# A cross-attention block on one core: a ring for the softmax weights, values copied by ScalarE, one DMA queue

## The chip, the core and the metric

The kernel runs on one core of a Trainium2 chip. TensorE (PE in the profile) multiplies matrices, VectorE (DVE) and GpSimd (POOL) work on elements, reductions and small transposes, ScalarE (ACT) does activations and copies, and DMA transfers are issued by SyncE (SP) or by ScalarE. Each engine runs its own instructions in the order in which they were written and waits for the others at semaphores. The metric is device time in microseconds (us) for one execution; lower is better.

## The reference

The input is x and a context c, each 128 sequences of 128 tokens with 256 features, in fp32. For each sequence the reference computes one cross-attention block with 16 heads of 16 features and a feed-forward layer of 1024:

```python
q = x @ Wq + bq;  k = c @ Wk + bk;  v = c @ Wv + bv        # 16 heads of 16
scores = q @ k.T / sqrt(16)
scores = where(j < i, scores, -1e30)                       # strictly below the diagonal
attn = softmax(scores);  attn[..., 0, :] = 0
x1 = layer_norm(x + (attn @ v) @ Wo + bo, ln1_g, ln1_b)
out = layer_norm(x1 + relu(x1 @ W1 + b1) @ W2 + b2, ln2_g, ln2_b)
```

## The kernel before

Two sequences make a pair, so there are 64 pairs. Several pairs are in flight at once: the main loop's `step(p)` (lines 988 to 1042, p from 5 to 63) computes the scores and the softmax of pair p, weighs the values of pair p-2 and takes them through the output projection and the first norm, runs the feed-forward layer of pair p-3, starts the second norm of pair p-4 and finishes and stores pair p-5. Nothing reorders the work: the order of calls in `step` is the order on each engine. Pairs 0 to 4 go through written-out openings (the last of them are `third`, `fourth` and `fifth`), and the last pairs through a written-out tail from line 1050 on.

On PE a step is: `weigh(p-2)` (lines 464 and 474), `scores_both(p)` (line 357), `queries(p+1)` and `keys(p+1)` (line 257), with `attention_out(p-2)` (line 493) between them, `values(p)` (line 289), `hidden(p-3)` (line 680) and `second(p-3)` (line 698). All eight PSUM banks are assigned by hand. Two assignments matter here. `second` leaves its result in bank 6, and the last part of the next step's `scores_both` writes to bank 6 too, so it cannot start before VectorE has read the result in `second_sum` (line 708). And `hidden` uses banks 2, 3, 4 and 0, which the next `scores_both` needs as well, so ScalarE must have run its Relu on them (line 686).

The scores are cut by query rows into a low half (rows 0 to 63 of each sequence, which see 64 keys) and a high half (rows 64 to 127, which see 128 keys). For each half VectorE adds the mask (`mask`, line 371) and takes the negated maximum (line 382), GpSimd adds it (line 383), ScalarE takes the exponential (line 390), VectorE sums and inverts (`sums`, lines 402 and 403) and GpSimd multiplies (line 404). The high half goes in two parts of eight heads, called ONE and TWO, the low half as a whole.

To weigh values, PE needs the weights turned, with keys on the partitions. VectorE transposes 32x32 blocks into a tile `tb` (`turn`, line 417, three instructions a pair), and sixteen DMA transfers then exchange the blocks between partition groups, from `tb` into `pT` (`bring`, line 432). The first-norm output takes a like road: a block transpose into `tbx` (`turn_x1`, line 644), four transfers to DRAM (line 235) and one back (line 238), for `hidden`.

The buffers: the scores have two tiles each for the low and high halves, `tb` one and `pT` one. So `turn(p)` must wait until `bring(p-1)` has read `tb`, and `bring(p-1)`, issued at the start of step p, may write `pT` only after `weigh(p-2)` has read it. `values_out` (lines 294 to 307) puts the values into zero-padded tiles: `vz` for the high rows and `vd` for the low ones, where the second head of a pair of heads lies on partitions 64 to 127. ScalarE copies the first half of `vd` from PSUM, and a DMA from `vz`, issued by ScalarE (line 303), fills the second half. `store` (line 587) is issued by ScalarE too. All other transfers of the loop are issued by SyncE.

The first norm's statistics are four VectorE instructions (`stats`, lines 506 and 507), a variance step on GpSimd (`deviation`, `shift`, lines 513, 514 and 558) and two ScalarE activations (`norm1`, line 535), which stand between the Relus of `hidden`. At two pairs `second` also issues idle PE instructions; that stays as it is.

Of the kernel before, what the change touches and what calls it, by code (L numbers as in the profile page):

```python
# [8 lines left out]
F32 = mybir.dt.float32  # L9
# [4 lines left out]
P = 128  # L14
# [5 lines left out]
def tile_cross_attention_block(  # L20
# [273 lines left out]
    def values_out(p):  # L294
        st = states[p]
        pv = st.pop("pv")
        st["vz"], st["vd"] = vzs[p % 2], vds[p % 2]
        for s in range(2):
            nc.scalar.copy(
                st["vz"][:, s, :, 0:4:3, :],  # L300
                pv[:, s * D : (s + 1) * D].rearrange("p (r e d) -> p r e d", e=2, d=DK),
            )
        nc.scalar.dma_start(st["vd"][HP:], st["vz"][:HP, :, :, 2:4, :])
        nc.scalar.copy(
            st["vd"][:HP, :, :, 0, :].rearrange("p s r d -> p (s r) d"),
            pv[:HP].rearrange("p (u e d) -> p u e d", e=2, d=DK)[:, :, 0, :],
        )

    def scores(p, hi):

        st = states[p]
        n = P if hi else HP
        sps = [at_bank(r, f"pss{hi}_{p}_{r}") for r in range(NS)]
        for m in range(KC):
            for s in range(2):
                first = s * P  # L320
                for r in range(NS):
                    strip = slice(32 * r, 32 * r + 32)
                    nc.tensor.matmul(
                        sps[r][
                            s * HP : (s + 1) * HP, m * 2 * n : (m + 1) * 2 * n
                        ].rearrange("p (e j) -> p e j", e=2),
                        st["qT"][strip, m, first + hi * HP : first + hi * HP + HP],
                        st["kT"][strip, m, :, first : first + n],
                        start=True, stop=True,
                    )  # L330
        st["sps", hi] = sps
        st["sm", hi] = soft.tile(
            [P, H, n], F32, tag=f"sm{hi}", name=f"sm{hi}_{p}", bufs=2
        )
        st["nmx", hi] = small.tile([P, H], F32, tag=f"nmx{hi}", name=f"nmx{hi}_{p}")

    def scores_both(p):

        st = states[p]
        for hi in range(2):  # L340
            st["sps", hi] = [
                at_bank(r if hi else (6, 7, 4, 5)[r], f"pss{hi}_{p}_{r}") for r in range(NS)
            ]
            st["sm", hi] = soft.tile(
                [P, H, P if hi else HP], F32, tag=f"sm{hi}", name=f"sm{hi}_{p}", bufs=2
            )
            st["nmx", hi] = small.tile([P, H], F32, tag=f"nmx{hi}", name=f"nmx{hi}_{p}")
        one, two = (0, 1), (2, 3)
        for strips, hi, m in (
            (two, 0, 0), (one, 1, 0), (two, 0, 1), (one, 1, 1),  # L350
            (two, 1, 0), (two, 1, 1), (one, 0, 0), (one, 0, 1),
        ):
            n = P if hi else HP
            for s in range(2):
                for r in strips:
                    strip, first = slice(32 * r, 32 * r + 32), s * P
                    nc.tensor.matmul(  # L357
                        st["sps", hi][r][
                            s * HP : (s + 1) * HP, m * 2 * n : (m + 1) * 2 * n
                        ].rearrange("p (e j) -> p e j", e=2),  # L360
                        st["qT"][strip, m, first + hi * HP : first + hi * HP + HP],
                        st["kT"][strip, m, :, first : first + n],
                        start=True, stop=True,
                    )
# [46 lines left out]
    def turn(p, hi, t):  # L411

        st = states[p]
        if "tb" not in st:
            st["tb"] = soft.tile([P, NS, (H + HH) * 32], F32, tag="tb", name=f"tb_{p}")
        at = (t if hi else 2) * 256
        nc.vector.transpose(  # L417
            st["tb"][:, :, at : at + 256].rearrange("p j (n a) -> p n j a", a=32),
            st["sm", hi].rearrange("p h j -> p (h j)")[:, t * 1024 : (t + 1) * 1024].rearrange(
                "p (n j a) -> p n j a", j=NS, a=32  # L420
            ),
        )

    def bring(p, queue, which):

        st = states[p]
        if "pT" not in st:
            pT = st["pT whole"] = soft.tile([P, NS, (H + HH) * 32], F32, tag="pT", name=f"pT_{p}")
            st["pT"] = pT.rearrange("p i (n a) -> p i n a", a=32)
        for u in which:  # L430
            i, j = u // NS, u % NS
            queue.dma_start(  # L432
                st["pT whole"][32 * j : 32 * j + 32, i, :], st["tb"][32 * i : 32 * i + 32, j, :]
            )

    def turn_on_pe(p, hi, ts):

        st = states[p]
        sm = st["sm", hi].rearrange("p h j -> p (h j)")
        if "pT" not in st:  # L440
            pT = soft.tile([P, NS, (H + HH) * 32], F32, tag="pT", name=f"pT_{p}")
            st["pT"] = pT.rearrange("p i (n a) -> p i n a", a=32)
        for t in ts:
            pt = bank(f"ptp{hi}_{p}_{t}")
            for i in range(4):
                at = (4 * t + i) * P
                nc.tensor.transpose(pt[:, i * P : (i + 1) * P], sm[:, at : at + P], ident)
            n = 4 * t if hi else H + 4 * t
            nc.scalar.copy(
                st["pT"][:, :, n : n + 4, :].rearrange("p i n a -> p n i a"),  # L450
                pt.rearrange("p (n i a) -> p n i a", i=NS, a=32),
            )
# [70 lines left out]
    def attention_stats(p):  # L523
        stats(p, states[p]["t1"], 1)
        deviation(p, 1)
# [58 lines left out]
        nc.vector.scalar_tensor_tensor(t2, t2, sd, be2_r, ALU.mult, ALU.add)  # L584

    def store(p):
        nc.scalar.dma_start(
            out[2 * p : 2 * p + 2].rearrange("b p d -> p b d"), states.pop(p)["t2"]
        )

# [323 lines left out]
    def fourth():  # L914
# [26 lines left out]
        turn(p, 1, 1)  # L941
        attention_out(p - 1)
        attention_sum(p - 1)
        sums(p, 0, ALL)
        attention_stats(p - 1)
        shift(p - 1, 1)
        tokens(p + 2, "x")
        keys(p + 1)
        turn(p, 0, 0)
        bring(p, nc.sync, LATE_FIRST)  # L950
        stats(0, states[0]["t2"], 2)
        scale_and_shift(0)
        norm1(p - 1)
        turn_x1(p - 1)
        hidden(1, range(FC))
        norm2(0)

    def fifth():
        p = 4
        load_ahead(p)  # L960
        scores_both(p)
        mask(p, 0, B)
        mask(p, 1, A)
        maximum(p, 1, ONE)
        queries(p + 1)
        mask(p, 1, B)
        maximum(p, 1, TWO)
        exponential(p, 1, ONE)
        mask(p, 0, A)
        maximum(p, 0, ALL)  # L970
        keys(p + 1)
        exponential(p, 1, TWO)
        values(p)
        values_out(p)
        sums(p, 1, ONE)
        exponential(p, 0, ALL)
        sums(p, 1, TWO)
        sums(p, 0, ALL)
        tokens(p + 2, "x")
        tokens(p + 2, "c")  # L980
        second(1, 0)
        second(1, 1)
        turn(p, 1, 0)
        turn(p, 1, 1)
        turn(p, 0, 0)
        hidden(2, range(FC // 2))

    def step(p):
# [1 line left out]
        weigh(p - 2)  # L990
        context(p - 2)
        scores_both(p)
        bring(p - 1, nc.sync, LATE_FIRST)
        load_ahead(p)
        second_sum(p - 4)
        residual1(p - 3)
        finish(p - 5)
        add_bo(p - 1)
        mask(p, 0, B)
        mask(p, 1, A)  # L1000
        maximum(p, 1, ONE)
        if not last:
            queries(p + 1)
        store(p - 5)
        attention_out(p - 2)
        mask(p, 1, B)
        maximum(p, 1, TWO)
        exponential(p, 1, ONE)
        mask(p, 0, A)
        maximum(p, 0, ALL)  # L1010
        if not last:
            keys(p + 1)
        exponential(p, 1, TWO)
        attention_sum(p - 2)
        values(p)
        stats(p - 4, states[p - 4]["t2"], 2)
        stats(p - 2, states[p - 2]["t1"], 1)
        scale_and_shift(p - 4)
        deviation(p - 2, 1)
        shift(p - 2, 1)  # L1020
        values_out(p)
        sums(p, 1, ONE)
        exponential(p, 0, ALL)
        sums(p, 1, TWO)

        def between(f):
            if f == 4:
                norm1(p - 2)

        hidden(p - 3, range(FC // 2 if p == 5 else 0, FC), between)  # L1030
        norm2(p - 4)
        sums(p, 0, ALL)
        if p + 2 < NP:
            tokens(p + 2, "x")
            tokens(p + 2, "c")
        turn(p, 1, 0)
        turn_x1(p - 2)
        turn(p, 1, 1)
        turn(p, 0, 0)
        pad = 7 if p in (28, 51) else 0  # L1040
        second(p - 3, 0, pad=pad)
        second(p - 3, 1, pad=pad)
# [7 lines left out]
    p = NP - 1  # L1050
    weigh(p - 1)
    context(p - 1)
    bring(p, nc.sync, LATE_FIRST)
    second_sum(p - 3)
    residual1(p - 2)
    finish(p - 4)
# [7 lines left out]
    scale_and_shift(p - 3)  # L1064
    store(p - 4)
    hidden(p - 2, range(2, FC), lambda f: norm1(p - 1) if f == 4 else None)
    turn_x1(p - 1, nc.scalar)
    norm2(p - 3)
    second(p - 2, 0)
    second(p - 2, 1)  # L1070
# [85 lines left out]
```

## Time and profile before

Three runs gave 1625.21, 1629.5 and 1635.55 us; the median is 1629.5 us.

| | |
|---|---|
| the profiled execution's own time | 1624.7 us |
| its span | 1623.0 us |
| PE busy, PE weight loads busy | 1588.8 us (98%), 1359.0 us (84%) |
| VectorE, GpSimd, ScalarE busy | 1266.6 us (78%), 1304.0 us (80%), 787.8 us (49%) |
| mean granted PE clock | 0.994 |
| DMA queue of SyncE, of ScalarE | 183.08 MB in 394912 packets, 26.50 MB in 86704 packets |
| VectorE idle before the turns (line 417) | 258.9 us |

The span is the time between the first and the last instruction in the trace. A matmul's end is modelled in the trace, and successive matmuls overlap, so PE's 98% is not a measure of how much work there was; the distance between the starts of the same instruction in two steps is the surer measure. In a list of waits, a line names the waiting engine and line, then what released it, then the total in us, the count and the longest. `PEld` is PE loading weights, and `SPq` is the queue of instructions by which SyncE issues transfers.

### The profile page before, as it was taken

The page shows a single profiled execution, that of the slowest core. Times are in us where ns is not written, and L with a number is a line of the kernel's source. Part 1 is how long each engine was busy: PE and PEld are TensorE (multiplying, and loading weights), DVE is VectorE, ACT ScalarE, POOL GpSimd, SP SyncE. Part 2 cuts the span into 40 slices and gives each one's busy share as a digit, 9 for nine tenths or more (in the row PEclk, how much of TensorE's full clock was granted, in tenths as well). Part 3 has the DMA queues.
Part 4 walks back from the last instruction along what each step waited for, and adds up shares of the span by engine and source line. Part 5 has one row for each costly group of instructions (what it writes and reads, how often), then busy time and mean ns, then how long its engine had stood idle before and what let it go on. Part 6 is the DMA issues. An engine that isn't in the chain of part 4 may idle for free.

```text
span 1623.0 us, 41609 instructions
## 1 busy us (share of the span) xinstructions
PE 1588.8 (98%) x16486; PEld 1359.0 (84%) x16486; DVE 1266.6 (78%) x2125; ACT 787.8 (49%) x1616; POOL 1304.0 (80%) x1229
## 2 busy tenths in 40 slices
PE   8989999999999999999999999999999999999998
PEld 7768888888888888888888888888888888888877
DVE  6967877878878778778778788787787787787852
ACT  5545445445445355354454454453554554544532
POOL 6859788788888787787887888887878878878873
PEclk9989999999999999999999999999999999999999
DMA  9435555565665665656655656656556656565541
GB/s 196 99 79 132 136 130 127 137 138 136 141 131 125 138 143 131 140 121 137 134 140 138 133 124 138 139 133 141 126 131 141 138 132 133 129 138 119 137 120 48
DMA packets 481809, 212.23 MB, mean 131 GB/s; under 512 B 349008, under 2 KB 449616, under 8 KB 481616
## 3 DMA queue, kind: packets, MB, share of 16 engines
q1 hardware_dynamic: 394912, 183.08, 50.3%
q10 hardware_dynamic: 86704, 26.50, 6.6%
q8 instruction: 131, 2.15, 0.6%
q14 instruction: 62, 0.51, 0.1%
HBM read 70.26 MB, written 33.29 MB: 64 GB/s over the span
## 4 chain that ended last, share of the span: by engine, by line
DVE 31%; DMA 16%; SPq 14%; PE 13%; ACT 13%; POOL 9%; issue 4%; DVEq 0%; ACTq 0%; POOLq 0%
SPq L432 14%; DVE tb L417 12%; DMA vd<-vz 9%; DVE sm L371 7%; DMA pT<-tb 6%; ACT sm L390 6%; POOL sm L383 6%; DVE nmx L382 5%; ACT kT L279 4%; PE ph L680 4%; PE py L698 3%; POOL sm L404 2%; DVE tbx L644 2%; DVE t L708 2%; DVE su L402 2%
## 5 line engine op out<-in xcount | busy, mean ns | idle before, releaser
L383 POOL TENSOR_TENSOR sm<-sm,nmx 128x1024 f32<-128x1024 f32 x192 | 364.3, 1898 | 234.2 <-DVE nmx L382 231.6
L680 PE MATMUL ph<-x1T,w 128*128 128x256 f32 x2048 | 455.8, 380 | 5.6 <-DMA x1T<-x1t 5.4
L698 PE MATMUL py<-w,hT 128*128 128x256 f32 x2016 | 446.1, 379 | 0.8 <-ACT hT L686 0.8
L680 PEld LDWEIGHTS ph<-x1T,w 128*128 128x128 f32 x2048 | 389.5, 191 | 60.8 <-issue 3.3
L698 PEld LDWEIGHTS py<-w,hT 128*128 128x128 f32 x2016 | 382.7, 190 | 54.3 <-ACT hT L686 2.4
L417 DVE STREAM_TRANSPOSE tb<-sm 128x1024 f32<-128x1024 f32 x186 | 221.9, 1217 | 258.9 <-DMA pT<-tb 142.6
L404 POOL TENSOR_TENSOR sm<-sm,rs 128x1024 f32<-128x1024 f32 x192 | 359.3, 1898 | 5.6 <-DVE rs L403 5.4
L371 DVE TENSOR_TENSOR sm<-pss,neg 128x512 f32<-128x512 f32 (+1 forms) x512 | 253.4, 545 | 17.6 <-PE pss L357 13.6
L390 ACT ACTIVATE sm<-sm 128x1024 f32<-128x1024 f32 x192 | 203.3, 1059 | 112.2 <-POOL sm L383 104.4
L382 DVE TENSOR_REDUCE nmx<-sm 128x8 f32<-128x1024 f32 (+1 forms) x192 | 234.3, 1220 | 6.6
L402 DVE TENSOR_REDUCE su<-sm 128x8 f32<-128x1024 f32 (+1 forms) x192 | 225.8, 1176 | 5.2 <-ACT sm L390 5.2
L486 ACT COPY cxT<-pc 128x508 f32<-128x508 f32 x64 | 37.3, 582 | 391.6 <-PE pc L474 391.6
L686 ACT ACTIVATE hT<-ph,b1e_c 128x256 f32<-128x256 f32 x504 | 202.4, 466 | 36.0 <-PE ph L680 33.0
L268 ACT ACTIVATE qT<-pq,bqs_c 128x256 f32<-128x256 f32 x126 | 52.8, 470 | 213.7 <-PE pq L257 213.7
L357 PE MATMUL pss<-kT,qT 32*64 32x256 f32 (+1 forms) x3840 | 129.0, 335 | 15.3 <-DVE t L708 10.6
L357 PEld LDWEIGHTS pss<-kT,qT 32*64 32x64 f32 x3840 | 89.3, 132 | 46.1 <-DVE t L708 32.0
L257 PE MATMUL pq<-xT,wq 128*128 128x256 f32 x504 | 127.3, 396 | 0.0
L279 ACT ACTIVATE kT<-pk,bkh,half 128x256 f32<-128x256 f32 x252 | 121.6, 563 | 4.4 <-PE pk L257 4.4
L493 PE MATMUL po<-wo,cxT 128*128 128x256 f32 x512 | 121.2, 379 | 0.0
L289 PE MATMUL pv<-wv,cT 128*128 128x256 f32 x512 | 121.0, 379 | 0.0
L257 PE MATMUL pk<-cT,wk 128*128 128x256 f32 x504 | 119.2, 379 | 0.0
L257 PEld LDWEIGHTS pq<-xT,wq 128*128 128x128 f32 x504 | 91.7, 192 | 20.8 <-issue 10.1
(100 smaller groups left out, 1814.7 us busy)
## 6 DMA issues: line engine op xcount, KB each, us to landing
pT<-tb SPq DMA_DIRECT2D x984, 96.0 KB, 2.2
out_dram<-t ACTq DMA_DIRECT2D x63, 256.0 KB, 2.5
xb<-in_x_dram SPq DMA_DIRECT2D x124, 128.0 KB, 3.7
cb<-in_ctx_dram SPq DMA_DIRECT2D x124, 128.0 KB, 3.7
x<-in_x_dram SPq DMA_DIRECT2D x31, 512.0 KB, 5.3
x1t<-tbx SPq DMA_DIRECT2D x248, 64.0 KB, 3.5
x1T<-x1t SPq DMA_DIRECT2D x62, 256.0 KB, 3.1
vd<-vz ACTq DMA_DIRECT2D x64, 128.0 KB, 2.8
```

The source lines that it names most:

```text
L257: nc.tensor.matmul(ps[:, m * TP : (m + 1) * TP], w[:, k, m * P : (m + 1) * P], src[:, k, :], start=(k == 0), stop=(k == KC - 1),)
L357: nc.tensor.matmul(st["sps", hi][r][s * HP : (s + 1) * HP, m * 2 * n : (m + 1) * 2 * n].rearrange("p (e j) -> p e j", e=2), st["qT"][strip ...
L371: nc.vector.tensor_tensor(st["sm", hi][:, 4 * r : 4 * r + 4, :], st["sps", hi][r][:, : 4 * n].rearrange("p (n j) -> p n j", j=n), no[:, No ...
L382: nc.vector.tensor_reduce(nmx[:, part], sm[:, part, :], AX.X, ALU.max, negate=True)
L383: nc.gpsimd.tensor_tensor(sm[:, part, :], sm[:, part, :], nmx[:, part, None].to_broadcast([P, part.stop - part.start, n]), ALU.add,)
L390: nc.scalar.activation(sm[:, part, :], sm[:, part, :], AF.Exp)
L402: nc.vector.tensor_reduce(su, sm[:, part, :], AX.X, ALU.add)
L404: nc.gpsimd.tensor_tensor(sm[:, part, :], sm[:, part, :], rs[:, :, None].to_broadcast([P, part.stop - part.start, n]), ALU.mult,)
L417: nc.vector.transpose(st["tb"][:, :, at : at + 256].rearrange("p j (n a) -> p n j a", a=32), st["sm", hi].rearrange("p h j -> p (h j)")[:, ...
L432: queue.dma_start(st["pT whole"][32 * j : 32 * j + 32, i, :], st["tb"][32 * i : 32 * i + 32, j, :])
L680: nc.tensor.matmul(ph[:, i * TP : (i + 1) * TP].rearrange("p (s i a) -> p s i a", s=2, a=32), w1[:, k, (f + i) * P : (f + i + 1) * P], st[ ...
L698: nc.tensor.matmul(st["py"][:, s * D : (s + 1) * D], st["hT"][:, f, s * P : (s + 1) * P], w2[:, f, :], start=(f == 0), stop=(f == FC - 1),)
```

## The change

Four things are changed together.

1. The scores of a pair (both halves in one tile, now named `sm`), its `tb` and its `pT` come from one ring of four equal buffers, `wide`, taken in the order in which they are first used. The space is the same as that of the tiles they replace.
2. The second half of `vd` is copied by ScalarE from PSUM, partitions 0 to 63, to partitions 64 to 127; the DMA goes.
3. `store` is issued by SyncE, and in the tail one `turn_x1` moves from ScalarE's queue to SyncE's. `bring(p)` is issued at the end of step p, after the turns, and no longer at the start of step p+1; `fifth` gets such a call, and the tail loses one. `load_ahead(p)` now stands after `store`.
4. `attention_sum`, the statistics, `deviation` and `shift` of the first norm (pair p-2) come ahead of the low half's maximum; `norm1` stands after the second group of Relus of `hidden` (f == 2) and not after the third (f == 4); `turn_x1` stands right after `hidden`, ahead of `sums(p, 0)`, of the token transposes and of the turns. `fourth` is changed likewise.

The diff's core, with the unchanged lines between left out:

```diff
-        nc.scalar.dma_start(st["vd"][HP:], st["vz"][:HP, :, :, 2:4, :])
-        nc.scalar.copy(
-            st["vd"][:HP, :, :, 0, :].rearrange("p s r d -> p (s r) d"),
-            pv[:HP].rearrange("p (u e d) -> p u e d", e=2, d=DK)[:, :, 0, :],
-        )
+        for e in range(2):
+            nc.scalar.copy(
+                st["vd"][e * HP : (e + 1) * HP, :, :, e, :].rearrange("p s r d -> p (s r) d"),
+                pv[:HP].rearrange("p (u e d) -> p u e d", e=2, d=DK)[:, :, e, :],
+            )
...
+    def wide(name):
+        return soft.tile([P, NS * (H + HH) * 32], F32, tag="wide", name=name, bufs=4)
+
+    def room(p, hi):
+        st = states[p]
+        if "sm" not in st:
+            st["sm"] = wide(f"sm_{p}")
+        at = H * P if not hi else 0
+        n = P if hi else HP
+        st["sm", hi] = st["sm"][:, at : at + H * n].rearrange("p (h j) -> p h j", j=n)
+        st["nmx", hi] = small.tile([P, H], F32, tag=f"nmx{hi}", name=f"nmx{hi}_{p}")
...
-            st["tb"] = soft.tile([P, NS, (H + HH) * 32], F32, tag="tb", name=f"tb_{p}")
+            st["tb"] = wide(f"tb_{p}").rearrange("p (j n) -> p j n", j=NS)
...
-            pT = st["pT whole"] = soft.tile([P, NS, (H + HH) * 32], F32, tag="pT", name=f"pT_{p}")
+            pT = st["pT whole"] = wide(f"pT_{p}").rearrange("p (i n) -> p i n", i=NS)
...
     def store(p):
-        nc.scalar.dma_start(
+        nc.sync.dma_start(
...
     def fourth():
...
-        sums(p, 0, ALL)
         attention_stats(p - 1)
         shift(p - 1, 1)
+        sums(p, 0, ALL)
         tokens(p + 2, "x")
         keys(p + 1)
+        hidden(1, range(FC), lambda f: norm1(p - 1) if f == 2 else None)
+        turn_x1(p - 1)
         turn(p, 0, 0)
         bring(p, nc.sync, LATE_FIRST)
         stats(0, states[0]["t2"], 2)
         scale_and_shift(0)
-        norm1(p - 1)
-        turn_x1(p - 1)
-        hidden(1, range(FC))
         norm2(0)
...
     def fifth():
...
         turn(p, 0, 0)
+        bring(p, nc.sync, LATE_FIRST)
         hidden(2, range(FC // 2))
...
     def step(p):
...
-        bring(p - 1, nc.sync, LATE_FIRST)
-        load_ahead(p)
         second_sum(p - 4)
         residual1(p - 3)
         finish(p - 5)
+        store(p - 5)
         add_bo(p - 1)
+        load_ahead(p)
...
-        store(p - 5)
...
         mask(p, 0, A)
+        attention_sum(p - 2)
+        attention_stats(p - 2)
+        shift(p - 2, 1)
         maximum(p, 0, ALL)
...
-        attention_sum(p - 2)
         values(p)
         stats(p - 4, states[p - 4]["t2"], 2)
-        stats(p - 2, states[p - 2]["t1"], 1)
         scale_and_shift(p - 4)
-        deviation(p - 2, 1)
-        shift(p - 2, 1)
...
         def between(f):
-            if f == 4:
+            if f == (FC // 2 if p == 5 else 2):
                 norm1(p - 2)
         hidden(p - 3, range(FC // 2 if p == 5 else 0, FC), between)
+        turn_x1(p - 2)
         norm2(p - 4)
         sums(p, 0, ALL)
...
         turn(p, 1, 0)
-        turn_x1(p - 2)
         turn(p, 1, 1)
         turn(p, 0, 0)
+        bring(p, nc.sync, LATE_FIRST)
...
-    bring(p, nc.sync, LATE_FIRST)
...
-    turn_x1(p - 1, nc.scalar)
+    turn_x1(p - 1)
```

More of the change, by code (lines that the diff above doesn't have):

```diff
@@ L331, in scores @@
         st["sps", hi] = sps
[L332 to L335, printed above, removed]
+        room(p, hi)
     def scores_both(p):
@@ L343, in scores_both @@
             ]
[L344 to L347, printed above, removed]
+            room(p, hi)
         one, two = (0, 1), (2, 3)
@@ L440, in turn_on_pe @@
         if "pT" not in st:
-            pT = soft.tile([P, NS, (H + HH) * 32], F32, tag="pT", name=f"pT_{p}")
+            pT = wide(f"pT_{p}").rearrange("p (i n) -> p i n", i=NS)
             st["pT"] = pT.rearrange("p i (n a) -> p i n a", a=32)
```

## The prediction

> **What bounds the kernel now.** I read the page's busy shares first, then the waits of the engines, then TensorE's timeline by steps, and last SyncE's own waits.
>
> ```profile
> PE 1588.8 (98%) x16486; PEld 1359.0 (84%) x16486; DVE 1266.6 (78%) x2125; ACT 787.8 (49%) x1616; POOL 1304.0 (80%) x1229
> ```
>
> PE looks full, which would leave 1623.0 - 1588.8 = 34 us to gain. That reading is wrong, because ends are modelled and overlapping matmuls hide a late one. The start of a step on PE is its first L464 line. Step 62 and an ordinary step, from PE's timeline:
>
> ```profile
> 729.96 0.43 PE L464 MATMUL pc<-pT,vd 128*32 128x64 f32 x16
> ...
> 731.43 1.57 PE L357 MATMUL pss<-kT,qT 32*64 32x128 f32 x48
> 734.25 0.67 PE L357 MATMUL pss<-kT,qT 32*64 32x128 f32 x16 [1.25 <-DVE t L708]
> ...
> 755.76 0.43 PE L464 MATMUL pc<-pT,vd 128*32 128x64 f32 x16
> ...
> 1520.30 0.43 PE L464 MATMUL pc<-pT,vd 128*32 128x64 f32 x16
> ...
> 1521.78 1.62 PE L357 MATMUL pss<-kT,qT 32*64 32x128 f32 x64
> 1523.33 1.99 PE L257 MATMUL pq<-xT,wq 128*128 128x256 f32 x8
> ...
> 1544.25 0.43 PE L464 MATMUL pc<-pT,vd 128*32 128x64 f32 x16
> ```
>
> The ordinary step takes 25.80 us, step 62 23.95. All pieces but the scores agree within 0.1 us; the scores go from 1.55 us to 3.4, because their last quarter waits until VectorE has emptied bank 6 (L708). From step 6 (136.64) to step 63 (1544.25) there are 57 steps in 1407.6 us, 24.70 each: 0.75 us above the step without a wait. The waits say the same, and why VectorE is late:
>
> ```profile
> DVE tb L417 <- DMA pT<-tb: 142.6, 31, 5.2
> ...
> DVE tb L417 <- POOL x1b L547: 101.5, 23, 4.7
> ...
> PEld pss L357 <- DVE t L708: 32.0, 52, 2.1
> ...
> PE pss L357 <- DVE t L708: 10.6, 23, 1.6
> ```
>
> The last two add up to 42.6 us, as 57 x 0.75 does. VectorE is late because the turns wait for `tb`. (Where GpSimd's L547 is named, it had no part: nothing in the turn reads its output; the landing of the transfers fell in that moment.) Then SyncE's own waits:
>
> ```profile
> SPq L432 <- DMA vd<-vz: 164.0, 56, 5.3
> SPq L432 <- DMA out_dram<-t: 96.4, 42, 4.8
> ```
>
> The sixteen transfers of `bring` stop for the two that ScalarE issues, 2.5 us each in the step at 705: they take 15.71 us there, 11.10 in step 62. So the loop is: late values and store hold up `bring`, that the turns, those `second_sum`, that PE.
>
> Two openings add a price that the busy share hides. PE's timeline, then its windows; the number after the count in brackets is the granted clock (0.62, 0.50, 0.74, 0.50):
>
> ```profile
> 90.24 0.52 PE L357 MATMUL pss<-kT,qT 32*64 32x128 f32 x8 [3.73 <-ACT hT L686]
> ...
> 110.25 5.41 PE L680 MATMUL ph<-x1T,w 128*128 128x256 f32 x16 [2.42 <-DMA x1T<-x1t]
> ```
>
> ```profile
> 90.00:92.00 2.00, 1.56 (x36) 0.62 0.67 160
> 92.00:94.00 2.00, 2.00 (x45) 0.50 0.56 139
> ...
> 110.00:112.00 2.00, 1.75 (x6) 0.74 1.23 150
> 112.00:114.00 2.00, 2.00 (x6) 0.50 0.50 52
> ```
>
> After each gap the clock is halved for a while: scores plus queries take 7.07 us from 90.24 instead of 3.38, and the half `hidden` 5.34 instead of 3.45. The clock thus cost 3.7 + 1.9 = 5.6 us beside the gaps. The Trainium skill, "TensorE: Matmul & The Clock Gate", Part 1, puts a warm-up at about 3.4 us at half rate, so some 1.7 us lost a time, 3.4 for both (an estimate from that page), and asks for idle gaps above about 3.4 us; here a gap of 2.42 was enough. The rows decide, and the sum below uses them alone.
>
> **The change, part by part.** Times t count from a step's start on PE, at a period of 23.95, with VectorE's and the other durations of the steps at 705 and 1520.
>
> *Queue and ring.* `bring` has 16 issues at 0.59 + 0.05 us, 10.2 us. SyncE's whole step becomes: store 0.4, loads 4 x 0.7 and half of 1.0 (3.3), x1t 4 issues 1.8 to 2.7, wait for their landing 1.4, x1T 0.4, bring 10.2: about 18.4 us of 23.95. Order: x1t at t = 18.2, x1T 22.2, `bring` 24.3 to 34.3, then store (its `finish` ended at t = 2.5) and loads until 14.3 of the next step, 4 us ahead of the next x1t. `pT` lands at 36.5 and is needed at 47.9, two starts later: 11 us of cover; if it went, `weigh` would wait for all that is missing. The ring asks for nothing new: `tb(p)` takes the scores of p-1, `pT(p)` the `tb` of p-1, whose reading ended at 12.6, and `sm(p+1)` the `pT` of p-2, read by `weigh` over 20 us earlier. The stored tile is written again at the next step's start, 10 us after the store has landed. Loads move by some 10 us; they are used a step later or more.
>
> *The copy.* ScalarE loses an idle 0.68 us around the DMA's issue and gains a copy. The trace has none across partitions: the lower bound is the neighbouring half's 0.27 us step, the upper the DMA's 2.8 us landing. I take 0.3, the nearest row (same shape, engine and source). It lies in ScalarE's wait for the low half's exponential, 12.2 to 13.9, so up to 1.9 us is free.
>
> *The norm.* The four statistics and the sum for pair p-2, 1.66 us, move ahead of the low half's maximum. VectorE: masks from 2.3, low mask done 8.7, sum and statistics 10.3, maximum 11.5, second norm's statistics 12.5, both high sums 15.2. GpSimd: high subtractions 5.6 to 9.9, `deviation` and `shift` 10.3 to 11.9, low subtraction 13.8. ScalarE: low exponential 14.9 (13.9 in step 62), Relus 0 to 3 by 16.5, `norm1` by 17.5 (17.2 in step 62, so it is not sooner at all), Relus 4 to 7 by 19.1. `second` starts at 16.9 and needs Relus 4 at 18.7 and 7 at 19.9: about 0.5 to 0.8 us to spare.
>
> VectorE now queues behind `turn_x1`: it idles 15.2 to 17.5, then `turn_x1` 18.2, low sums 19.5, tokens 20.7, turns 21.9, 23.0, 24.2 (GpSimd's three products end at 17.4, 19.3, 21.4 and hold up none). `second_sum` runs 0.3 to 0.9 into the next step; it must end by 2.3, where the step at 705 began to stall. So 1.4 us to spare, and PE is the bound: 57 steps at 23.95 = 1365.2 instead of 1407.6, **-42.4** (0.9 of it is one wait of `weigh` for pT at 161).
>
> *Opening.* In `fourth`, Relus 0 to 3 no longer wait for `norm1` (86.92): ScalarE is free at 83.7, Relus 4 and 5 end at 87.0, 6 and 7 at 87.8. Scores start at 87.1 with a further 0.7 of wait and end at 89.2 at full clock, instead of 93.7. x1T lands at 93.5, before `hidden(2)` at 101.5. Step 5 starts at 105.0, not 115.6. But it has only half a `hidden` and catches VectorE (`second_sum` ends at 108.5): I count 1.1 us at the scores and 1.5 for late Relus, step 6 at 128.1 instead of 136.6: **-8.5**.
>
> *Tail.* Step 63 has no projections ahead of `hidden`, so the later exponential shows: Relu 0 at 15.3 instead of 13.9, `second` ends at 23.2 instead of 21.6. The wait of 2.97 us for x1T goes, since it lands at 25.2 and was waited for until 26.1: **-0.9**.
>
> Sum -51.8: span 1571, the run 1573 against this execution's own 1624.7. The median shown, 1629.5, is 4.8 above that execution; 1629.5 - 51.8 = **1578**.
>
> A rule speaks against the change: the Trainium skill, "Perfetto Trace Analysis", DMA Optimizations, advises spreading issues over the engines where issuing is the limit. By it, store on SyncE would cost its 0.4 us a step, 23 us in all, if SyncE set the period. The rows have SyncE at 18.4 of 23.95 and the two queues' waits at 164.0 + 96.4 us, so I count that at nothing.
>
> **The rivals.**
>
> 1. *VectorE is still late in part* (0.17). `turn_x1` now stands ahead of low sums, tokens and turns; if `norm1` or the sums come 1.4 us later than I count, PE waits again. For: three engines hand over in turn. Against: 2.3 us of its idle time lies there already. The commonest short steps of before stall 0.35 us; at that price 57 x 0.35 = 20: 1598.
>
> 2. *The wait changes its name* (0.08). The sixteen transfers stop for others on the same queue, and the steady steps stay at 24.70: 1578 + 42 = 1620, within 1%. For: SyncE already waits 2.8 us for x1t ahead of x1T. Against: `bring` now has 11 us of cover.
>
> 3. *SyncE sets the pace, slower* (0.10). If store, loads and x1t, now all ahead of `bring`, each stop the queue 2.5 us, as the two foreign transfers did, 18.4 + 7.5 = 25.9 a step, 1.2 above 24.70: 1629.5 - 9 + 57 x 1.2 = 1689. It decides from 6.3 us of such waits a step. Against: eight of sixteen issues at 0.64 outlast a landing of 2.2 us, and in the trace none of the queue's own transfers delayed `bring` for more than 3.4 us in all.
>
> **How the numbers follow.** Chances: forecast 0.65, rivals 0.17, 0.08, 0.10. About 1% is what a measurement here can tell from no change. Faster by over 1% are the forecast and rival 1, 0.82; within 1% rival 2, 0.08; slower 0.10. The range takes in the forecast and rival 1: from 1566 (the runs as near the span as this profile's, all steps at 23.95, and the 2.6 us counted in step 5 and 2 in the tail gone) to 1604 (rival 1 and 6 us, the half of a runs' spread of 10); the rest is 0.18. The forecast's own range is 1566 to 1588.
>
> **What would show it.** Steps of about 23.95 us between L464 starts, no wait of PE's scores for L708, no turn waiting for pT<-tb, SyncE's waits for vd<-vz and out_dram<-t gone, a 0.3 us second copy, and clock 1.00 around 90 and 112. Rival 1 shows as PE waits for L708 with VectorE held at `turn_x1`; rival 2 as transfers of 15 us and `weigh` waiting for pT; rival 3 as x1T late at `hidden`. I am wrong if VectorE's slack of 1.4 us is spent.

## The result, and the profile after

The changed kernel takes 1572.55 us (median of 4 runs, 1572.12 to 1572.94). Against the kernel before on the same chip (1629.17 us, median of 4 runs) the ratio is 0.9649, with a 95% interval of 0.9618 to 0.968. The profiled execution took 1572.12 us, its span is 1570.3 us. Forecast were 1578 us, with a range of 1566 to 1604.

From the pages: the shares, by engine, of the chain that ended last in the kernel before, then the busy shares, the same chain and the line of the turns in the kernel after:

```profile
DVE 31%; DMA 16%; SPq 14%; PE 13%; ACT 13%; POOL 9%; issue 4%; DVEq 0%; ACTq 0%; POOLq 0%
```

```profile
PE 1554.3 (99%) x16486; PEld 1347.3 (86%) x16486; DVE 1273.2 (81%) x2125; ACT 802.7 (51%) x1680; POOL 1304.3 (83%) x1229
...
PE 89%; DVE 3%; SPq 3%; DMA 2%; issue 1%; POOL 1%; ACT 0%; ACTq 0%; POOLq 0%; DVEq 0%
...
L424 DVE STREAM_TRANSPOSE tb<-sm 128x1024 f32<-128x1024 f32 x186 | 214.5, 1203 | 0.2
```

The busy share of PE rose by one point, from 98% to 99%, and its busy time fell by 34.5 us; the span fell by 52.7. The chain tells more: it ran over PE for 13% of the span before and for 89% after, and of the loop of DMA, turns and sum little is left in it. VectorE's idle time ahead of the turns fell from 258.9 us to 0.2. One step, from PE's timeline of the kernel after:

```profile
701.77 0.43 PE L471 MATMUL pc<-pT,vd 128*32 128x64 f32 x16
...
703.25 1.62 PE L364 MATMUL pss<-kT,qT 32*64 32x128 f32 x64
704.80 1.99 PE L257 MATMUL pq<-xT,wq 128*128 128x256 f32 x8
...
725.72 0.43 PE L471 MATMUL pc<-pT,vd 128*32 128x64 f32 x16
```

The scores run through in 1.55 us, and the step takes 23.95 us. So do all steps from 6 to 62 but two: 23.94 or 23.95 by their starts. The two are those with the idle PE instructions, 24.87 and 24.85. (Lines have moved by 7: L464 is now L471, L357 L364, L417 L424, L708 L715.)

The same step on VectorE:

```profile
701.91 0.66 DVE L715 TENSOR_TENSOR t<-py,x1b 128x512 f32<-128x512 f32 x1
704.06 1.95 DVE L378 TENSOR_TENSOR sm<-pss,neg 128x256 f32<-128x256 f32 x4 [1.48 <-PE pss L364]
...
719.29 0.71 DVE L651 STREAM_TRANSPOSE tbx<-x 128x512 f32<-128x512 f32 x1 [2.27 <-DMA xb<-in_x_dram]
...
722.48 3.46 DVE L424 STREAM_TRANSPOSE tb<-sm 128x1024 f32<-128x1024 f32 x3
725.86 0.66 DVE L715 TENSOR_TENSOR t<-py,x1b 128x512 f32<-128x512 f32 x1
```

VectorE now waits for PE ahead of the masks (1.48 us), where PE waited for VectorE before. The three turns run back to back, and L715 starts 0.14 us after the step's start, at once behind the last turn. The 2.27 us at L651 are the wait for `norm1`; the transfer named there has nothing to do with it, it landed in that moment. On ScalarE:

```profile
713.56 0.75 ACT L304 COPY vd<-pv 64x256 f32<-64x256 f32 x2
715.78 1.06 ACT L397 ACTIVATE sm<-sm 128x1024 f32<-128x1024 f32 x1 [1.46 <-POOL sm L390]
...
718.17 1.10 ACT L542 ACTIVATE x<-t,nb,sd 128x256 f32<-128x256 f32 x2
```

Both value copies take 0.75 us together, and 1.46 us of waiting follow them. `norm1` ends at 719.27, 17.5 us into the step, as it was forecast. SyncE's queue in the same step:

```profile
702.02 11.58 SPq L439 DMA_DIRECT2D pT<-tb  x16
713.71 0.52 SPq L594 DMA_DIRECT2D out_dram<-t  x1
714.28 4.36 SPq L92 DMA_DIRECT2D xb<-in_x_dram  x4
720.03 1.78 SPq L235 DMA_DIRECT2D x1t<-tbx  x4
723.26 0.38 SPq L238 DMA_DIRECT2D x1T<-x1t  x1
```

The sixteen transfers, store, loads and x1t follow one another, and 1.4 us lie between the loads' end and x1t.

### The profile page after: what moved, and what is told of

It reads as the page before. It is cut to its first block, busy times and chain, and to the rows that moved or that the text cites. A ratio compares the mean times of both kernels' runs of the same rounds, so it can differ in the third digit from the quotient of the medians.

```text
span 1570.3 us, 41807 instructions
## 1 busy us (share of the span) xinstructions
PE 1554.3 (99%) x16486; PEld 1347.3 (86%) x16486; DVE 1273.2 (81%) x2125; ACT 802.7 (51%) x1680; POOL 1304.3 (83%) x1229
## 4 chain that ended last, share of the span: by engine, by line
PE 89%; DVE 3%; SPq 3%; DMA 2%; issue 1%; POOL 1%; ACT 0%; ACTq 0%; POOLq 0%; DVEq 0%
PE ph L687 26%; PE py L705 25%; PE pq L257 7%; PE po L500 6%; PE pk L257 6%; PE pv L289 6%; PE pss L364 5%; PE pc L481 3%; PE pc L471 2%; SPq L439 2%; DVE tb L424 1%; DVE sm L378 1%; DMA x<-in_x_dram 1%; SPq L92 1%; DVE nmx L389 1%
## 5 line engine op out<-in xcount | busy, mean ns | idle before, releaser
L411 POOL TENSOR_TENSOR sm<-sm,rs 128x1024 f32<-128x1024 f32 x192 | 361.7, 1898 | 24.8 <-DVE rs L410 24.7
L424 DVE STREAM_TRANSPOSE tb<-sm 128x1024 f32<-128x1024 f32 x186 | 214.5, 1203 | 0.2
L693 ACT ACTIVATE hT<-ph,b1e_c 128x256 f32<-128x256 f32 x504 | 197.7, 479 | 24.7 <-PE ph L687 24.7
L651 DVE STREAM_TRANSPOSE tbx<-x 128x512 f32<-128x512 f32 x63 | 44.8, 712 | 139.1 <-ACT x L542 95.9
L500 PEld LDWEIGHTS po<-wo,cxT 128*128 128x128 f32 x512 | 97.1, 190 | 13.7 <-ACT cxT L493 0.3
L289 PEld LDWEIGHTS pv<-wv,cT 128*128 128x128 f32 x512 | 97.2, 190 | 13.2
```

The lines of the kernel that those rows point to most:

```text
L289: nc.tensor.matmul(pv[:, s * D : (s + 1) * D], st["cT"][:, k, s * P : (s + 1) * P], wv[:, k, :], start=(k == 0), stop=(k == KC - 1),)
L411: nc.gpsimd.tensor_tensor(sm[:, part, :], sm[:, part, :], rs[:, :, None].to_broadcast([P, part.stop - part.start, n]), ALU.mult,)
L424: nc.vector.transpose(st["tb"][:, :, at : at + 256].rearrange("p j (n a) -> p n j a", a=32), st["sm", hi].rearrange("p h j -> p (h j)")[:, ...
L500: nc.tensor.matmul(po[:, s * D : (s + 1) * D], cxT[:, k, s, :], wo[:, k, :], start=(k == 0), stop=(k == KC - 1),)
```

## The experiments

The theory: lateness went round a loop (two transfers on ScalarE hold up `bring`, that the turns, those `second_sum`, that PE), and only what exceeded VectorE's cover reached PE. Rivals: the single buffers are the cause whatever the queue; each part of the change earns its own share; the norm's new order earns nothing; VectorE is at its limit now. Eleven kernels were run. Of each the median is given, the ratio to the kernel before on the same chip, and the mean of the steps 6 to 62 from PE's timeline (24.70 before, 23.98 after).

**The queue alone.** The kernel before, with the copy and the queue of `store`:

```diff
-        nc.scalar.dma_start(st["vd"][HP:], st["vz"][:HP, :, :, 2:4, :])
...
+        for e in range(2):
+            nc.scalar.copy(... st["vd"] of half e ... pv ...)
...
-        nc.scalar.dma_start(out[2 * p : 2 * p + 2] ...
+        nc.sync.dma_start(out[2 * p : 2 * p + 2] ...
```

> The kernel before with only the second values copy on ScalarE and store on SyncE; buffers, place of bring, norm order and opening as before. Theory (one late chain: bring is held up, then the turns, then second_sum, then PE): without the two waits of 2.5 us bring runs from t = 6.1 behind x1T to 16.5 and lands at 18.5 of a step, when VectorE reaches the turns at 18.1, so the turns are 0.4 us late at most, PE waits no more, steps are 23.95 us, and the time is 1629 - 42 = 1587 us. Rival (the single buffers are the cause, whatever queue the transfers take): turns still wait for pT<-tb, steps stay near 24.7, 1629 us. Rival (the parts add up): something between, 1600 to 1615 us.

Measured: 1576.12 us, ratio 0.9684 (0.9668 to 0.9701), steps of 23.95. The wait of VectorE that has grown, from 16.2 us before, in the list of waits of this kernel:

```profile
DVE t L708 <- PE py L698: 124.0, 59, 6.1
```

VectorE waits 2 us a step for PE ahead of `second_sum`. The single `tb` and `pT` do not matter once the queue is free: the rival with the buffers falls. The time is 11 us below what was expected. In the profile 6.0 us of that lie in the opening, which gained too (below), and the tail took 2.3 back; most of the rest is the starting point, as 1629 us lay 4.8 above the execution from which the 42 us were read.

**The buffers alone.** The ring, and `bring` at the end of its own step; both transfers stay on ScalarE:

```diff
     def step(p):
...
-        bring(p - 1, nc.sync, LATE_FIRST)
...
         turn(p, 0, 0)
+        bring(p, nc.sync, LATE_FIRST)
```

> The kernel before with only the ring of four buffers and bring at the end of its own step (load_ahead stands a little later); values and store transfers stay on ScalarE, norm order and opening as before. Theory: bring has 11 us of cover and two waits of 2.5 us do not use it up, no turn waits for bring, steps are 23.95 us, 1587 us. Rival (the two queues' waits are the cause): SyncE's step is 18.4 + 5 = 23.4 us and slips in some steps, x1T or pT comes late, 1600 to 1629 us.

Measured: 1580.61 us, ratio 0.9715 (0.9699 to 0.9731), steps of 23.94. SyncE's own waits in this kernel:

```profile
SPq L92 <- DMA vd<-vz: 163.3, 55, 3.8
...
SPq L439 <- DMA out_dram<-t: 47.0, 51, 5.1
```

The wait for the values is as long as before, 163.3 us, now at the loads; it costs nothing, because nobody needs those transfers soon. So either part alone brings the steady steps to PE's own pace. The parts do not add up; each is enough.

**One transfer alone.** Two kernels: before with the copy and `store` left on ScalarE, and before with `store` on SyncE and the values DMA left.

> The kernel before with only the second values copy on ScalarE in place of its DMA; store stays on ScalarE, all else as before. Theory (a threshold: lateness costs only what exceeds VectorE's cover): bring runs from t = 6.1 with one wait of 2.5 us, lands at 21.0, second_sum ends at 1.7 of the next step, ahead of 2.3, so PE hardly waits and almost the whole gain of both transfers is there: 1576 to 1582 us. Rival (each transfer earns its 2.5 us of 5): half the gain, 1600 us.

> The kernel before with only store issued by SyncE, behind bring and the loads; the values DMA stays on ScalarE. Theory (threshold): one wait of 2.5 us is left, as in the other half, so steps fall to about 24 us; the opening keeps its wait for the values DMA and its slow clock, 1583 to 1588 us. Rival (each transfer earns its 2.5 us of 5): 1600 us. Rival (only the values DMA matters, as it comes last and lands last): 1625 us.

Measured: 1575.94 us, ratio 0.9692 (0.9665 to 0.9719), steps of 23.95, with the copy; 1585.41 us, ratio 0.9745 (0.9716 to 0.9775), steps of 23.97, with the store. From the waits of the kernel with the copy, SyncE's and VectorE's:

```profile
SPq L432 <- DMA out_dram<-t: 210.4, 55, 5.1
```

```profile
DVE tb L417 <- DMA pT<-tb: 34.5, 37, 1.8
```

The wait for `store` has more than doubled, from 96.4 to 210.4 us, and the turns still wait 34.5 us; PE waits for L708 no more. So it was not the length of the waits that counted. A step of the kernel with the copy, PE's first line and SyncE's:

```profile
705.57 0.43 PE L464 MATMUL pc<-pT,vd 128*32 128x64 f32 x16
```

```profile
707.68 14.91 SPq L432 DMA_DIRECT2D pT<-tb  x16
```

The sixteen transfers still take 14.7 us from the first issue to the last on the mean of the steady steps, and took 14.9 before. But they start 2.0 us into the step and not 6.4, as x1T is issued at 0.8 and not at 5.8, and the last lands at 18.3 and not at 22.9 (at 14.5 in the kernel with both edits). That is the threshold: 4.6 us of those 8.4 take the whole loss of the steady steps away. Of the 9.5 us between the two kernels 6.5 lie in the opening, where they need 130.6 and 137.1 us up to step 6; 2.1 lie in the tail. The kernel with the values DMA has this wait of SyncE in front of x1t there, which the one with the copy lacks:

```profile
SPq L235 <- DMA vd<-vz: 6.6, 1, 6.6
```

**The norm's order alone.** The kernel before with the main step's new order:

```diff
+        attention_sum(p - 2)
+        attention_stats(p - 2)
+        shift(p - 2, 1)
         maximum(p, 0, ALL)
...
-            if f == 4:
+            if f == (FC // 2 if p == 5 else 2):
                 norm1(p - 2)
...
         hidden(p - 3, range(FC // 2 if p == 5 else 0, FC), between)
+        turn_x1(p - 2)
```

> The kernel before with only the new order in the main step of statistics, norm1 and turn_x1; buffers, queues, bring and opening as before. Theory: x1t and x1T are issued before the step's end and no longer stand in front of bring, so bring can start at t = 1.5 right after weigh has read pT instead of at 6.1; with the two waits of 2.5 us it lands at about 19, before VectorE reaches the turns at 20.7; PE waits no more, 1587 us. Rival (this order earns nothing in the steady steps, since norm1 itself is not sooner): 1629 us, or up to 20 us more, as VectorE is held at turn_x1.

Measured: 1601.52 us, ratio 0.9841 (0.9826 to 0.9855), steps of 24.31. Both theories missed: a part of the gain is there. The waits of VectorE and, behind them, SyncE's:

```profile
DVE tbx L644 <- ACT x L535: 138.7, 62, 2.3
...
DVE tb L417 <- DMA pT<-tb: 65.6, 38, 2.9
```

```profile
SPq L432 <- DMA vd<-vz: 153.8, 55, 3.8
SPq L432 <- DMA out_dram<-t: 90.0, 34, 5.1
```

The foreign transfers still hold up `bring`. I had it starting at t = 1.5; in the step at 669.00 it starts at 675.83, t = 6.8, since x1t still stands in front of it in SyncE's queue, and had itself waited behind the late transfers of the step before and the loads. VectorE's whole idle time ahead of the turns fell from 258.9 to 95.2 us, 65.6 of it put down to the transfers, but it now idles 138.7 us ahead of `turn_x1`. Behind the turns' wait 0.7 us less of VectorE's work stands ahead of `second_sum`, as `turn_x1` is already done; that fits the 0.39 us a step, but was not tried by itself.

**All but the norm's order.** The changed kernel with the main step's order of before; `fourth` stays changed.

> The changed kernel with the main step's order of statistics, norm1 and turn_x1 as before (the opening's keeps the new order). Theory: ring and queue alone keep VectorE in time, steps stay 23.95 us, 1572 to 1574 us; the last full step gets its low exponential 1.3 us sooner. Rival (each part has its share of the gain): 1580 to 1590 us.

Measured: 1571.17 us, ratio 0.9658 (0.9642 to 0.9674), steps of 23.95. The order earns nothing in the main loop once the other parts are there. It even has a price: the two steps with the idle PE instructions take 23.94 and 24.16 us here, and 24.87 and 24.85 in the changed kernel; in the four kernels with the old order above (the queue, the ring, the copy, the store alone) both take 23.94, and in the one with the norm's order alone 25.46 and 24.87. Step 63 takes 21.34 us here and 23.28 in the changed kernel, but the wait for x1T behind it, 2.71 us, is back. Why the idle instructions cost 0.9 us a step only beside the new order stays open.

**The opening step in the old order.** The changed kernel with `fourth` as before:

```diff
     def fourth():
...
-        hidden(1, range(FC), lambda f: norm1(p - 1) if f == 2 else None)
-        turn_x1(p - 1)
...
+        norm1(p - 1)
+        turn_x1(p - 1)
+        hidden(1, range(FC))
```

> The changed kernel with the opening step (fourth) in the order of before. Theory: the two gaps at 86 and 108 us come back with the halved clock behind them, 3.9 + 2.4 us of gaps and 3.7 + 1.9 us of slow clock, while the steady steps stay at 23.95 us: 10 to 11 us more than the changed kernel, 1583 us. Rival (the opening's price is the gaps alone, the clock costs nothing further): 6 us more, 1578 us. Rival (the late start is made up by the later steps): 1573 us.

Measured: 1575.62 us (1572.7 to 1577.39), ratio 0.9687 (0.9669 to 0.9705), steps of 23.98. All three expectations missed: it costs 3 us by the medians, which come from two chips, and 0.6 by the profiled execution, the fastest of the four. From the starts of `weigh(2)` to `weigh(3)` it needs 35.4 us, the changed kernel 32.8, the kernel before 43.6. The gap at the scores is there again, but x1T comes in time, and the clock was another one. PE's line and its windows (granted clock behind the count in brackets) of this kernel, and then of the queue alone, which has the same order in `fourth`:

```profile
86.88 0.45 PE L364 MATMUL pss<-kT,qT 32*64 32x128 f32 x8 [2.49 <-ACT hT L693]
```

```profile
88.00:90.00 2.00, 2.00 (x56) 1.00 0.65 157
90.00:92.00 2.00, 2.00 (x11) 1.00 0.51 126
```

```profile
88.74 3.57 PE L357 MATMUL pss<-kT,qT 32*64 32x128 f32 x64 [2.62 <-ACT hT L686]
```

```profile
88.00:90.00 2.00, 1.23 (x27) 0.65 0.64 157
90.00:92.00 2.00, 2.00 (x52) 0.50 0.52 126
```

A gap of 2.49 us left the clock at 1.00, one of 2.62 us at the same place halved it for some 7 us, and in the kernel before one of 2.42 us did. In the tail of the kernel with all but the norm's order a gap of 2.71 us left it at 1.00 too. So the gap's length alone does not decide. The Trainium skill, "TensorE: Matmul & The Clock Gate", Part 1, says that the activity window is free-running, so that the same kernel meets it in another phase each time; the runs agree with that (this kernel's four times spread over 4.7 us, those of the changed kernel, which has no such gap there, over 0.8), but none isolates it.

**VectorE's spare time.** The changed kernel with one, or two, more reductions a step ahead of the turns, whose result nobody reads:

```diff
+        for i in range(1):        # 2 in the second kernel
+            more = small.tile([P, HH], F32, tag="more", ...)
+            nc.vector.tensor_reduce(more, states[p]["sm", 1][:, ONE, :], AX.X, ALU.add)
         turn(p, 1, 0)
```

> The changed kernel with one more VectorE reduction of 128x1024 in each main step, ahead of the turns, into a tile that nobody reads; 1.15 us each, 68 us of added VectorE work in all. Theory (VectorE has about 1.5 us to spare before bank 6 is needed): no change, 1572 to 1574 us. Rival (VectorE is at its limit): 59 x 1.15 = 68 us more, 1640 us.

> The changed kernel with two more such VectorE reductions a step, 2.3 us. Theory: 2.3 us is 0.8 us over the 1.5 us to spare, so PE waits for L708's successor 0.8 us a step: 59 x 0.8 = 47 us more, 1620 us; VectorE idles 2.3 us at turn_x1, which does not help, as it lies ahead of the added work. Rival (2.3 us of that idle time is to spare as well): no change.

Measured: 1573.3 us, ratio 0.9675 (0.9657 to 0.9692) with one, steps of 24.00; 1611.93 us, ratio 0.9918 (0.9897 to 0.9939) with two, steps of 24.68. Some 69 us of VectorE work are free, about as much again costs 39. With two, an undisturbed step takes 24.62, 0.68 more than 23.94. The two hold up the turns by 2.22 us (714.53 to 716.75 in the step at 693.14), so 2.22 - 0.68 = 1.54 us were to spare, and the old wait is back in the list:

```profile
PEld pss L364 <- DVE t L715: 30.5, 55, 2.0
```

**Two small leftovers.** The changed kernel without the idle PE instructions and with the low maximum first in the last full step; and a kernel with the latter alone:

```diff
+        if last:
+            maximum(p, 0, ALL)
         attention_sum(p - 2)
         attention_stats(p - 2)
         shift(p - 2, 1)
-        maximum(p, 0, ALL)
+        if not last:
+            maximum(p, 0, ALL)
...
-        pad = 7 if p in (28, 51) else 0
+        pad = 0
```

> The changed kernel without the idle PE instructions at two pairs, and with the low maximum ahead of the first norm's sum in the last full step. Theory: two steps lose 0.92 us each and the last full step's Relus come 1.3 us sooner, 3 us less than the changed kernel, 1569.5 us. Rival (without the idle instructions something else goes late, or the clock falls): 1573 us or more.

> The changed kernel with one edit, in the last full step alone: the low maximum stands ahead of the first norm's sum; the idle PE instructions stay. Theory (the later low exponential delays that step's Relus and second): 1.8 us less than the changed kernel's 1572.5, 1570.7 us. Rival (the tail waits for something else next): 1572.5 us.

Measured: 1572.72 us, ratio 0.9668 (0.9652 to 0.9684) with both edits, no gain; 1569.82 us, ratio 0.9658 (0.9634 to 0.9681) with the last step's alone. That step falls from 23.28 to 21.47 us, the 1.8 expected; PE's line in the changed kernel, which the other one has without the wait:

```profile
1508.32 1.99 PE L705 MATMUL py<-w,hT 128*128 128x256 f32 x8 [1.75 <-ACT hT L693]
```

1569.82 is the lowest median of all kernels run here, though its distance to the changed kernel rests on runs of two chips, and in the profiles on that step for 1.8 us of 2.3. Without the idle instructions, PE stops in four steps where the profile shows nothing to wait for:

```profile
681.25 1.67 PE L257 MATMUL pq<-xT,wq 128*128 128x256 f32 x7 [0.59 <-issue]
705.49 0.37 PE L364 MATMUL pss<-kT,qT 32*64 32x128 f32 x2 [0.60 <-issue]
730.86 0.44 PE L364 MATMUL pss<-kT,qT 32*64 32x128 f32 x5 [1.10 <-issue]
755.67 0.45 PE L364 MATMUL pss<-kT,qT 32*64 32x128 f32 x8 [0.49 <-issue]
```

Five steps there take 24.26 to 25.43 us, 4.4 us in all over 23.94, against 1.8 us that the two padded steps cost. What these gaps are stays open.

## Why the prediction was right, point by point

| term | forecast | measured | from |
|---|---|---|---|
| opening, to step 6 | -8.5 | -10.5 | 126.19 against 136.64 |
| steps 6 to 62 | -42.4 | -40.9 | 1366.66 against 1407.61 |
| tail, from step 63 | -0.9 | -1.3 | 77.45 against 78.75 |
| sum | -51.8 | -52.7 | 1570.3 against 1623.0 |

*The steady steps* came out as worked: PE at 23.95, with the timeline of VectorE, GpSimd and ScalarE within 0.3 us (`turn_x1` at 17.5, turns from 20.7 to 24.2, `bring` from 24.2). The 1.5 us less than forecast are two steps of about 24.86: I had taken the idle PE instructions as unchanged, and the runs show a price for them beside the norm's new order alone, which the sum does not have. VectorE's 1.4 us to spare were 1.54 by the run with two reductions. The copy at 0.3 us is 0.37 us as a single instruction, 0.75 for both, inside the wait it was put in.

*That the busy share was no bound* held: 52.7 us were gained where 34 us looked idle.

*The cause* held, and its form was sharper than the forecast said. It listed copy, queue, ring and norm as parts of one sum; the runs show a threshold, where any one of copy, queue of `store`, or ring with an earlier `bring` brings the steady steps to 23.94 to 23.97. The sum did not need to know this, as it had all of them. The norm's order alone gives half of it, and none on top of the others.

*The opening* failed in its step: "Relus 0 to 3 no longer wait for `norm1`" and x1T "before `hidden(2)`" were both put down to `fourth`. The sum was near, the owner wrong, and that the sum came out is in part luck. With the old `fourth`, x1T comes in time too; what had held it up was the values DMA, in front of x1t (6.6 us in the kernel that keeps it). The new order of `fourth` is worth 2.6 us from `weigh(2)` to `weigh(3)`, and what the clock takes on top when a gap meets it; in the changed kernel it stayed at 1.00 from 86 to 126 us. Step 5 took 21.7 us, and not 23.1: I had counted 1.5 us for late Relus, and PE waited 0.57.

*The tail* was right in both halves: step 63's `second` ended at 23.28 for 23.2 forecast, and the wait for x1T is gone; x1T landed 24.7 us into step 63 and not at 25.2, which is the 0.4 us more.

*From the sum to the time* was the largest miss, 4.4 of the 5.4 us. I added the 4.8 us by which the median of before stood above its profiled run. After the change the four runs lie within 0.8 us, and the median is 0.4 above the profiled run. What spread the times of before was not tried by itself. In its 21 runs beside the experiments, on three chips, the span goes with the mean granted clock: 1618.9 us at 0.996, 1628.3 at 0.991, where 0.001 of the span is 1.6 us. The changed kernel's four runs have 0.999. In the profile of before the clock falls only up to 115 us and in the last 4 us. So most of the spread looks like the clock behind gaps and not like the loop, though the steps of that one execution range from 23.94 to 26.19 us.

*The rule against one queue* ("Perfetto Trace Analysis", DMA Optimizations, in the Trainium skill) did not apply, as counted: SyncE's queue is far busier than ScalarE's ever was, and still ends before x1t. But the margin I gave as 4 us is 1.4 in the step shown.

*Rivals.* Rival 1 (VectorE late in part) did not come; it begins some 1.5 us further on. Rival 2 (the wait changes its name) is seen in the kernel with the ring alone, where the wait goes on and costs nothing. Rival 3 (SyncE sets the pace) did not come.

## What to carry to other kernels

Measure a loop by the distance between the starts of the same instruction, take the shortest undisturbed step as its floor, and multiply the difference by the steps: that gave 42 us where busy shares gave 34 for the whole kernel. Where lateness passes from queue to engine to engine, find the cover at the end of the chain before adding up the delays: here transfers that landed 4.6 us sooner were worth as much in the steady steps as 8.4, and then 1.1 us more work was free while 2.2 was not. When transfers of two queues share completion semaphores, the one that is issued late holds up the other queue; give the hurried queue no such neighbour, or the transfer so much time that it does not matter.

## What the runs showed that was not expected

*Eight completion semaphores serve both DMA queues in turn.* The kept trace of the kernel before gives, for each transfer, the number of the semaphore that tells its landing, and of those that its issuer waits for. There are eight, 100 to 105, 107 and 108; each tells the landing of 195 to 204 transfers of SyncE and of 13 to 23 of ScalarE. Where one is still taken, the next transfer that is to use it waits. From the step at 704.16:

| issued at | by | transfer | semaphore | landed at |
|---|---|---|---|---|
| 711.15 | ScalarE | `store` | 107 | 714.82 |
| 714.84 | SyncE | `bring`, second of sixteen | 107 | 716.93 |
| 717.96 | ScalarE | values | 104 | 721.26 |
| 721.28 | SyncE | `bring`, eighth of sixteen | 104 | 723.91 |

So `bring` waited not for the data of the values but for the landing of the transfer that held its semaphore.

*Some issues take about 2 us, and more of them after the change.* The median of an issue of `bring` is 0.59 us before and after, and the longest 1.95 and 2.11, but from 161 us to 1480 us 22 of them take over 1 us before and 92 after. In the step shown one of the sixteen takes 2.06 us and one of the loads 2.12, together 2.9 us over their medians; the margin of 4 us lost 2.6. A fuller queue is not the reason by itself: with the copy alone or the ring alone SyncE issues no more transfers than before, and 68 and 76 take over 1 us. Why it happens was not tried.

*The clock was halved behind gaps of 2.42, 2.62 and 3.73 us and not behind gaps of 2.49 and 2.71.* Each halving lasted 3 to 7 us.
